# First token of each longer LSTM as seven block products instead of twelve plain ones, with VectorE's side work moved behind the first state

## The chip, the cores and the metric

One core of a Trainium2 chip runs the whole kernel. A core has five engines that each work through their own queue in order: TensorE (PE) multiplies 128x128 weight blocks with a stream of columns and writes to PSUM, VectorE (DVE) adds and multiplies elementwise, ScalarE (ACT) evaluates sigmoid, tanh and copies, GpSimd (POOL) does slower elementwise work, and SyncE (SP) issues DMAs. They wait for one another on semaphores. The metric is device time in microseconds (us); the kernel before takes 1878.06 us, the median of 3 runs (1877.81 to 1878.57).

## The reference, cut to what matters

Four residual layers work on x of shape (128 batches, 64 positions, 256 channels): a graph convolution with batch norms, then a graph convolution followed by windowed LSTMs, then two attention layers. The change concerns the LSTMs of the second layer alone:

```python
for p in range(1, MAX_SKIP + 1):                      # MAX_SKIP = 4
    nw = Tv // p
    wins = h[:, :nw * p, :].reshape(Bv * nw, p, Hd)
    last = _lstm_last(Wih[p-1], Whh[p-1], bih[p-1], bhh[p-1], wins)
    h = h.at[:, jnp.arange(nw) * p + (p - 1), :].set(last.reshape(Bv, nw, Hd))

def step(carry, x_t):                                 # in _lstm_last, from zero h and c
    h, c = carry
    g = x_t @ Wih.T + h @ Whh.T + bias
    i, f, gg, o = jnp.split(g, 4, axis=-1)
    c = sigmoid(f) * c + sigmoid(i) * tanh(gg)
    h = sigmoid(o) * tanh(c)
```

Positions are cut into windows of p tokens, an LSTM runs over each window, and its last state replaces the window's last position. The four LSTMs follow one another, since each reads what the one before wrote. At the first token h and c are zero, so only x_t @ Wih.T of the three gates i, g and o is needed.

## The kernel before

The 128 batches are worked on in eight pairs of chunks, "superchunks" sc = 0 to 7. Each holds 16 batches x 64 positions as a tile hT of 128 partitions x 2 channel blocks (k) x 1024 columns. For one superchunk the generator `lstms` runs p = 1 (`single`) and then `lstm` for p = 2, 3, 4. An LSTM with window p has n = 512, 336 or 256 columns for p = 2, 3, 4, and halves of m = n/2 = 256, 168 or 128 columns.

**Seven products.** A gate's 256x256 weight times its n columns is a 2x2 block product. The kernel already computes it for p = 1 and for all later tokens in Winograd's form of Strassen's method: seven products of 128x128 weights (or sums of weights) with m columns (or differences of columns) in place of eight, and some additions. The kinds are numbered 1 to 7. Kinds 1, 2 and 3 take columns as they are; 5, 6, 7 and 4 take the differences that `differences` makes (POOL for the x side in `operands_x`, VectorE for the h side, tile hd). The results are put together by copies (ScalarE, out of PSUM) and additions (VectorE, one operand out of PSUM). Weight sums are made once per (p, gate) in `weight_sums` (L744), kept in DRAM and loaded as tiles `wset` by `load_sets`; a set holds the x side, then the h side.

**The first token before** (L1106 to L1138) is the exception: for each of the gates 0, 2, 3 (i, g, o) and each output block c it sums two plain products (k = 0, 1) of n columns in its own PSUM bank: 12 products. All six with k = 0 come first, then a yield, then the six with k = 1. Six activations `first_acts` (L1113) read the banks, then come the cell c = 0 (L1119), its tanh (L1120), c = 1, and for each c the state h (`new_state`, L1093, tile hs). Between and behind the two states VectorE makes the h differences: dh[0] (L313) needs the state of c = 0 alone, dh[1] and dh[2] (L314 to L316) need both.

**The tokens after it** (class `Unit`, products at L1155, additions at L1164) start with the x parts of kinds 5, 3 and 2 for gates 0 and 2; after a yield come the h part of kind 5 (which reads dh[0]), copies, kind 1, and so on.

**Order of the work around it.** The order of instructions on each engine is written out by hand. PSUM has the tags x, y and z with two banks each for the LSTMs, and ps with two for everything else. `lstms` yields marks: a plain yield moves a counter n to the next whole number (a "tick"), a yield of "a" adds a half. In a superchunk p = 1 has ticks 0 to 3; p = 2 starts with 4 (in the middle of the first token's products) and 5 (after the x parts of the next token); p = 3 has 8 and 9 and p = 4 has 14 and 15 in these two places, and 21 is the end. At each tick the loop near the end of the LSTM part advances other generators by one step, as tuples of ticks say: CONV, BEGUN and FIRST (graph convolutions of coming chunks), RESIDUAL (adding the finished LSTM output, with a way through DRAM), AHEAD, LATE and FINAL (first norm of the attention layer), IDLE (idle transposes in the last superchunk, which has no convolutions).

The steps of a convolution that matter here, in order: scaled; transposes and DMA (L988, L247, L254, L995); add_squares (L284, VectorE, after that DMA); ln_stats (L159, L160); two applies (L196, ScalarE); aggregate "b" (L214, PE); two copies of its banks (L1005, VectorE); product_v (L915, PE, reads those copies); bounded (L921, VectorE); product_u (L929, PE, reads what bounded wrote); biased (L935, VectorE); aggregate "c" (L214, PE, reads what biased wrote); two steps of ScalarE (L940).

Before the change, for the chunk with an even number, both copies stand at tick 4 and product_v at tick 5; biased at tick 8 and aggregate "c" at tick 9. For the odd chunk bounded stands at tick 14 and product_u at tick 15. On VectorE, ticks 4, 8 and 14 lie ahead of everything of the first token but its products.

Of the kernel before, what the change touches and what calls it, by code (L numbers as in the profile page):

```python
# [13 lines left out]
P = 128  # L14
# [5 lines left out]
def kernel(  # L20
# [666 lines left out]
    with tc.manual_schedule(engines={mybir.EngineType.PE}):  # L687
# [56 lines left out]
        def weight_sums(p, q):  # L744
# [10 lines left out]
            far = dram.tile([P, 15, P], F32, tag=f"ws{p}{q}", name=f"wfar_{p}_{q}", bufs=1)  # L755
            nc.sync.dma_start(far[:, :9], w[:, :9])
            nc.sync.dma_start(far[:, 9:], w[:, 10:])
# [125 lines left out]
    def load_sets(n):  # L883
        for _ in range(min(n, len(coming))):
            p, q = coming.pop(0)
            wsets[p, q] = w1.tile([P, 15, P], F32, tag="wset", name=f"wset_{p}_{q}", bufs=6)
            nc.sync.dma_start(wsets[p, q], wfar[p, q])
# [136 lines left out]
    BLOCKS = {1: (0, 8), 2: (2, 9), 3: (7, 14), 4: (3, 10), 5: (4, 11), 6: (5, 12), 7: (6, 13)}  # L1024
# [14 lines left out]
    def operands_x(p, hv, name, s):  # L1039
# [3 lines left out]
        t = l1.tile([P, 7 * (T // 3) * NB], F32, tag="xd", name=f"xd_{name}_{s}", bufs=2)  # L1043
# [6 lines left out]
    def lstm(p, hv, name, follows, x1, ending):  # L1050
# [39 lines left out]
        def new_state(s, c, part, engine=nc.vector):  # L1090
# [6 lines left out]
            else:  # L1097
# [8 lines left out]
        ox = {1: x1}  # L1106

        banks = {(q, c): bank(f"g{q}_{name}_{c}", tag) for q, tag in ((0, "y"), (2, "z"), (3, "x"))
                 for c in range(KD)}
        def first_acts(*qs):  # L1110
            for q in qs:
                for c in range(KD):
                    nc.scalar.activation(  # L1113
                        columns_of(gate(q, c)),
                        natural(banks[q, c][:, :n].rearrange("p (w b) -> p w b", b=nb)),
                        AF.Tanh if q == 2 else AF.Sigmoid, bias=bs[:, q * KD + c : q * KD + c + 1])

        def first_cell(c):
            nc.vector.tensor_mul(cells[:, c, :n], gate(0, c), gate(2, c))  # L1119
            nc.scalar.activation(gate(2, c), cells[:, c, :n], AF.Tanh)  # L1120

        products = [(q, c, k) for k in range(KD) for q in GATES[:3] for c in range(KD)]
        for at, (q, c, k) in enumerate(products):
            if at == 6:
                yield
            nc.tensor.matmul(  # L1126
                banks[q, c][:, :n].rearrange("p (w b) -> p w b", b=nb), wsets[p, q][:, 2 * k + c, :],
                hv[:, k, : (nw - 1) * p + 1 : p, :], start=(k == 0), stop=(k == KD - 1))
# [961 lines left out]
```

## Time and profile before

| what | value |
|---|---|
| median of 3 runs | 1878.06 us |
| the profiled execution | 1879.19 us, its span 1877.4 us, granted TensorE clock 0.999 |
| PE busy | 1847.4 us, 98% of the span |
| DVE, ACT, POOL busy | 1245.6, 1014.0, 550.2 us |
| one middle superchunk (586 to 741 us) | 155.0 us, PE 153.58, DVE 103.33, ACT 86.63, POOL 36.19 us busy |
| first-token products (L1126), 576 records | 184.1 us busy, 474 ns mean |
| products of later tokens, x and y from differences of x (L1155) | 256.9 us and 77.5 us busy |

A product in fp32 stands in the trace as two records of matmul. The records overlap: a record's duration counts its way through the array, so the pace is read from the starts of neighbours. In the timeline, twelve records of 128x512 take 5.15 us to the start of the next group (429 ns each), and records of 128x256, 128x168 and 128x128 follow at 216, 142.5 and 111.7 ns. A group in the timeline shows its start, its length, engine, line, and in brackets the idle time before it with what ended it.

### The profile page before, as it was taken

To read this page: it belongs to the slowest core of one execution; us is meant where nothing else is said; L and a number is where in the kernel's file an instruction comes from. 1 tells how busy PE (TensorE), PEld (TensorE's weight loads), DVE (VectorE), ACT (ScalarE), POOL (GpSimd) and SP (SyncE) were. 2 spreads that over 40 slices of the span, in tenths; PEclk is the share of its full clock that TensorE was granted. 3 is DMA by queue.
4 is the path that set the end of the run, shared out by engine and by line. 5 is a ranking of instruction groups with operands and counts; after the bars stand their busy time and mean duration, and the time that the engine had idled before them with its cause. 6 is when DMAs were issued, how large, how long until landed. Compare 5 with 4: busy or idle time off the path is not lost.

```text
span 1877.4 us, 39077 instructions
## 1 busy us (share of the span) xinstructions
PE 1847.4 (98%) x15077; PEld 1476.8 (79%) x15077; DVE 1245.6 (66%) x3150; ACT 1014.0 (54%) x2284; POOL 550.2 (29%) x704
## 2 busy tenths in 40 slices
PE   8999989999999999999999999999999999999998
PEld 6877856895897798699589689778968967777776
DVE  6768855566577666667666766666565567776776
ACT  5766635556456456555655645655565544444453
POOL 5855722122222212212322312222132114332232
PEclk9999999999999999999999999999999999999999
DMA  3223652134334433332433443343144254444433
GB/s 115 71 70 141 238 200 92 66 129 152 107 130 147 145 141 127 113 136 95 150 119 132 165 137 130 130 132 125 60 142 140 70 157 136 145 149 139 144 113 114
DMA packets 111273, 241.45 MB, mean 129 GB/s; under 512 B 11504, under 2 KB 74864, under 8 KB 111088
## 3 DMA queue, kind: packets, MB, share of 16 engines
q1 hardware_dynamic: 110192, 237.09, 37.6%
q8 instruction: 119, 1.95, 0.4%
q0 software_dynamic: 320, 1.05, 0.2%
q10 hardware_dynamic: 576, 0.82, 0.1%
q14 instruction: 66, 0.54, 0.1%
HBM read 170.50 MB, written 68.42 MB: 127 GB/s over the span
## 4 chain that ended last, share of the span: by engine, by line
PE 86%; DVE 6%; DMA 2%; ACT 2%; issue 1%; POOL 1%; SPq 0%; DVEq 0%; ACTq 0%
PE x L1155 20%; PE z L1155 10%; PE g L1126 9%; PE v L1580 5%; PE y L1155 5%; PE x L1340 4%; PE y L1340 3%; PE v L915 3%; PE u L929 3%; PE p_q L1587 3%; PE X L1776 3%; PE X L423 2%; PE X L499 2%; PE Y L1776 1%; PE Y L423 1%
## 5 line engine op out<-in xcount | busy, mean ns | idle before, releaser
L1155 PE MATMUL x<-xd,wset 128*128 128x128 f32 (+2 forms) x1152 | 256.9, 305 | 8.6 <-DVE gates L1164 8.4
L1155 PE MATMUL x<-hd,wset 128*128 128x128 f32 (+2 forms) x1152 | 255.3, 303 | 0.0
L1221 POOL TENSOR_TENSOR gates<-gates 128x512 f32<-128x512 f32 (+2 forms) x48 | 75.2, 1566 | 534.4 <-ACT gates L1084 534.4
L1084 ACT ACTIVATE gates<-gates,bias 128x256 f32<-128x256 f32 (+4 forms) x384 | 172.4, 488 | 103.7 <-DVE gates L1164 103.7
L1164 DVE TENSOR_TENSOR gates<-gates,x 128x128 f32<-128x128 f32 (+2 forms) x384 | 120.7, 321 | 144.8 <-PE x L1155 141.6
L1164 DVE TENSOR_TENSOR gates<-gates,z 128x128 f32<-128x128 f32 (+2 forms) x384 | 102.6, 319 | 150.3 <-PE z L1155 150.1
L1155 PEld LDWEIGHTS x<-xd,wset 128*128 128x128 f32 x1152 | 188.2, 192 | 16.6 <-DVE gates L1164 11.6
L1155 PEld LDWEIGHTS x<-hd,wset 128*128 128x128 f32 x1152 | 188.5, 192 | 5.0
L1126 PE MATMUL g<-hT,wset 128*128 128x256 f32 (+2 forms) x576 | 184.1, 474 | 0.1
L1126 PEld LDWEIGHTS g<-hT,wset 128*128 128x128 f32 x576 | 108.6, 190 | 68.1 <-issue 37.8
L1161 ACT COPY gates<-y 128x128 f32<-128x128 f32 (+2 forms) x192 | 53.9, 293 | 197.4 <-PE y L1155 195.6
L1155 PE MATMUL z<-hT,wset 128*128 128x128 f32 (+2 forms) x768 | 146.7, 303 | 0.0
L1155 PE MATMUL z<-hs,wset 128*128 128x128 f32 (+2 forms) x768 | 146.5, 303 | 0.2 <-DVE hs L1093 0.2
L1155 PEld LDWEIGHTS z<-hT,wset 128*128 128x128 f32 x768 | 117.3, 191 | 3.7
L1155 PEld LDWEIGHTS z<-hs,wset 128*128 128x128 f32 x768 | 117.2, 191 | 3.6 <-DVE hs L1093 0.3
L1113 ACT ACTIVATE gates<-g,bias 128x512 f32<-128x512 f32 (+2 forms) x144 | 74.9, 560 | 38.1 <-PE g L1126 37.5
L1084 ACT ACTIVATE gates<-x,bias 128x128 f32<-128x128 f32 (+2 forms) x192 | 75.0, 390 | 30.1 <-PE x L1155 27.7
L1155 PE MATMUL x<-hT,wset 128*128 128x128 f32 (+2 forms) x384 | 86.0, 306 | 0.2 <-ACT gates L1084 0.2
L1155 PE MATMUL x<-hs,wset 128*128 128x128 f32 (+2 forms) x384 | 84.9, 303 | 0.0
L1236 ACT ACTIVATE gates<-cell 128x256 f32<-128x256 f32 (+2 forms) x144 | 55.2, 383 | 48.4 <-DVE cell L1235 48.4
L1155 PE MATMUL y<-hd,wset 128*128 128x128 f32 (+2 forms) x384 | 79.7, 310 | 0.0
L1155 PE MATMUL y<-xd,wset 128*128 128x128 f32 (+2 forms) x384 | 77.5, 304 | 1.8 <-ACT gates L1113 1.8
(326 smaller groups left out, 4120.9 us busy)
## 6 DMA issues: line engine op xcount, KB each, us to landing
wset<-wfar SPq DMA_DIRECT2D x96, 960.0 KB, 6.5
hT<-far_h SPq DMA_DIRECT2D x124, 128.0 KB, 3.1
far_h<-hm SPq DMA_DIRECT2D x16, 512.0 KB, 2.8
far_n<-xs SPq DMA_DIRECT2D x16, 512.0 KB, 3.5
xs<-far_n SPq DMA_DIRECT2D x64, 128.0 KB, 4.6
far_x<-xs SPq DMA_DIRECT2D x16, 512.0 KB, 3.0
x<-far_x SPq DMA_DIRECT2D x64, 128.0 KB, 3.2
xt<-in_x_dram SPq DMA_DIRECT2D x15, 512.0 KB, 4.0
```

The source lines that it names most:

```text
L423: nc.tensor.matmul(self.banks[tag][:, i * CH // 2 : (i + 1) * CH // 2], w, self.at[kind], start=first and not i, stop=True, skip_group_che ...
L915: nc.tensor.matmul(banks[m], wg0_sb[:, k, m * P : (m + 1) * P], agg[:, k, :], start=(k == 0), stop=(k == KD - 1))
L929: nc.tensor.matmul(banks[j // 2][:, j % 2, :], v[:, k, j * P : (j + 1) * P], wg1_sb[:, k, :], start=(k == 0), stop=(k == KD - 1))
L1084: nc.scalar.activation(gate(q, c, part), src, AF.Tanh if q == 2 else AF.Sigmoid, bias=bs[:, q * KD + c : q * KD + c + 1])
L1113: nc.scalar.activation(columns_of(gate(q, c)), natural(banks[q, c][:, :n].rearrange("p (w b) -> p w b", b=nb)), AF.Tanh if q == 2 else AF. ...
L1126: nc.tensor.matmul(banks[q, c][:, :n].rearrange("p (w b) -> p w b", b=nb), wsets[p, q][:, 2 * k + c, :], hv[:, k, : (nw - 1) * p + 1 : p, ...
L1155: nc.tensor.matmul(folded(self.psum(kind)), wsets[p, self.q][:, BLOCKS[kind][i], :], (ox[self.s] if part == "x" else oh)[kind], start=firs ...
L1164: nc.vector.tensor_add(gate(self.q, *dst), gate(self.q, *a), self.psum(kind))
L1221: nc.gpsimd.tensor_mul(gates[:, 0, :, :n], gates[:, 0, :, :n], gates[:, 2, :, :n])
L1340: nc.tensor.matmul(folded(ps(g, kind)), wih1[:, g, KINDS1[kind], :], right[kind], start=kind in (2, 5, 1), stop=True, skip_group_check=True)
L1580: nc.tensor.matmul(ps[:, i, :], hT[:, k, j, :], w[:, k, first : first + D], start=(k == 0), stop=(k == KD - 1))
L1776: nc.tensor.matmul(st[c, tag][:, i * CH // 2 : (i + 1) * CH // 2].rearrange("p (a n) -> p a n", n=P), w, st[c, "o7"][kind], start=first an ...
```

## The change

For p = 2, 3, 4 the first token is made of seven products as well. The class `First` holds one gate; `all_first` runs each step over the three gates. A gate has two banks: kinds 1 and 2 (and later 6, 7, 4 over kind 1's half) in one, 5 and 3 in the other, with the tags "yz", "yz", "xx". The x operands of token 0 are made by `operands_x` beside those of token 1 (four more POOL operations per LSTM), and the tile xd gets smaller and has three buffers in place of two. The second plain weight block is no longer needed, so a weight set shrinks from 15 to 14 blocks (three DMAs write it instead of two).

The yields of the first token are now: one after kinds 1 and 5, a half mark "a" behind the first state and dh[0], and the old one after the x parts of the next token, which now run in the order 3, 2, 5. The tuples of ticks change with it: what stood at ticks 4, 8 and 14 on VectorE now stands at 4.5, 8.5 and 14.5; add_squares of the odd convolution moves from 19 to 21; transposes of the second RESIDUAL from 2 to 1; several steps of AHEAD, FINAL and RESIDUAL move by one to four ticks.

```diff
-            far = dram.tile([P, 15, P], F32, tag=f"ws{p}{q}", name=f"wfar_{p}_{q}", bufs=1)
-            nc.sync.dma_start(far[:, :9], w[:, :9])
-            nc.sync.dma_start(far[:, 9:], w[:, 10:])
+            far = dram.tile([P, 14, P], F32, tag=f"ws{p}{q}", name=f"wfar_{p}_{q}", bufs=1)
+            for at, n, src in ((0, 1, 0), (1, 7, 2), (8, 6, 10)):
+                nc.sync.dma_start(far[:, at : at + n], w[:, src : src + n])
...
-        t = l1.tile([P, 7 * (T // 3) * NB], F32, tag="xd", name=f"xd_{name}_{s}", bufs=2)
+        t = l1.tile([P, 2 * CH], F32, tag="xd", name=f"xd_{name}_{s}", bufs=3)
...
-        products = [(q, c, k) for k in range(KD) for q in GATES[:3] for c in range(KD)]
-        for at, (q, c, k) in enumerate(products):
-            if at == 6:
-                yield
-            nc.tensor.matmul(
-                banks[q, c][:, :n].rearrange("p (w b) -> p w b", b=nb), wsets[p, q][:, 2 * k + c, :],
-                hv[:, k, : (nw - 1) * p + 1 : p, :], start=(k == 0), stop=(k == KD - 1))
-        first_acts(0, 2)
-        first_cell(0)
-        first_acts(3)
-        first_cell(1)
-        for c in range(KD):
-            new_state(0, c, every)
-            if not c:
-                dh[0]()
+        class First:
+            def __init__(self, q, tags):
+                self.q, self.ps = q, [bank(f"{t}{q}_{name}_{i}", t) for i, t in enumerate(tags)]
+            def psum(self, kind):
+                return self.ps[kind in (5, 3)][:, m:n] if kind in (2, 3) else self.ps[kind in (5, 3)][:, :m]
+            def product(self, kind):
+                nc.tensor.matmul(folded(self.psum(kind)), wsets[p, self.q][:, BLOCKS[kind][0], :], ox[0][kind],
+                                 start=kind in (1, 5), stop=True, skip_group_check=True)
+            def copy(self, c, j, kind):
+                nc.scalar.copy(gate(self.q, c, halves[j]), self.psum(kind))
+            def add(self, dst, a, kind):
+                nc.vector.tensor_add(gate(self.q, dst[0], halves[dst[1]]),
+                                     gate(self.q, a[0], halves[a[1]]), self.psum(kind))
+        firsts = [First(q, tags) for q, tags in ((0, "yz"), (2, "yz"), (3, "xx"))]
...
+        all_first(made(1), lambda u: u.copy(0, 0, 1), made(5), lambda u: u.copy(1, 1, 5))
+        yield
+        all_first(made(2), lambda u: u.add((0, 0), (0, 0), 2), made(3), made(6), lambda u: u.add((0, 1), (1, 1), 6),
+                  lambda u: u.add((0, 1), (0, 1), 3), made(7), lambda u: act(u.q, 0, every, gate(u.q, 0)),
+                  lambda u: u.add((1, 1), (1, 1), 7), made(4),
+                  lambda u: act(u.q, 1, halves[1], gate(u.q, 1, halves[1])))
+        nc.vector.tensor_mul(cells[:, 0, :n], gate(0, 0), gate(2, 0))
+        nc.scalar.activation(gate(2, 0), cells[:, 0, :n], AF.Tanh)
+        all_first(lambda u: act(u.q, 1, halves[0], u.psum(4)))
+        new_state(0, 0, every)
+        dh[0]()
+        yield "a"
+        nc.vector.tensor_mul(cells[:, 1, :n], gate(0, 1), gate(2, 1))
+        nc.scalar.activation(gate(2, 1), cells[:, 1, :n], AF.Tanh)
+        new_state(0, 1, every)
         dh[1]()
         dh[2]()
...
         A = [Unit(q, 1) for q in (0, 2)]
-        each(A, pe(5, "x"), pe(3, "x"), pe(2, "x"))
+        each(A, pe(3, "x"), pe(2, "x"), pe(5, "x"))
         yield
...
-                operands[p + 1] = operands_x(p + 1, hv, names[p + 1], 1)
+                operands[p + 1] = {s: operands_x(p + 1, hv, names[p + 1], s) for s in range(2)}
...
-    RESIDUAL = (0, 3, 4), (2, 5, 5.5)
-    CONV = (3, 4, 4, 5, 5.5, 7, 8, 9, 10, 10), (3, 4, 4, 11, 11.5, 13, 14, 15, 15.5, 17, 18, 20)
-    BEGUN = (11, 11, 13, 14, 16), (17, 17.5, 19)
...
-    AHEAD = (4, 5, 7, 12, 14, 15), (6, 7)
-    LATE = 5, 6, 8, 9
...
-    FINAL = (4, 5, 10, 12, 12, 14), (6, 7, 11, 14, 14, 16)
+    RESIDUAL = (0, 3, 5.5), (1, 5, 7)
+    CONV = (4, 4.5, 5, 5.5, 7, 8.5, 9, 10, 10), (3, 5, 5.5, 11, 11.5, 13, 14.5, 15, 15.5, 17, 18, 20)
+    BEGUN = (11, 11, 13, 15, 16, 17), (17, 17.5, 21)
...
+    AHEAD = (6, 7, 9, 12, 15, 19), (8, 9)
+    LATE = 5, 6, 9, 9.5
...
+    FINAL = (6, 7, 9.5, 10, 12, 13), (8, 9, 11.5, 12, 15, 15.5)
```

(FIRST, the tuple of the first superchunk, places the same steps at the same half ticks.)

## The prediction

> **What bounds the kernel now.** I read the page's busy times, then who waits for whom on PE, then the groups by form, then the timeline of one superchunk engine by engine.
>
> ```profile
> PE 1847.4 (98%) x15077; PEld 1476.8 (79%) x15077; DVE 1245.6 (66%) x3150; ACT 1014.0 (54%) x2284; POOL 550.2 (29%) x704
> ```
>
> ```profile
> PE x L1155 <- DVE gates L1164: 8.4, 13, 1.8
> ```
>
> ```profile
> L1126 PE MATMUL g<-hT,wset 128*128 128x512 f32 x192 | 85.6, 596 | 0.0
> ...
> L1126 PE MATMUL g<-hT,wset 128*128 128x336 f32 x192 | 55.7, 447 | 0.0
> ...
> L1126 PE MATMUL g<-hT,wset 128*128 128x256 f32 x192 | 42.8, 380 | 0.1
> ```
>
> PE is the bound: busy for 98% of the span; the second line, its largest group of waits, comes to 8.4 us in all. So a product saved is time saved, but every wait that the change puts in front of PE is lost in full. The last three rows are what is replaced: 192 records of each size in eight superchunks, 24 per LSTM.
>
> The timeline of superchunk 1 (start, length, group) shows how little air there is. PE first, then VectorE, for p = 2, 3 and 4:
>
> ```profile
> 450.12 5.31 PE L1126 MATMUL g<-hT,wset 128*128 128x512 f32 x12
> ...
> 464.30 3.60 PE L915 MATMUL v<-cv,wg_sb 128*128 128x512 f32 x8
> 467.73 1.03 PE L1155 MATMUL y<-hd,wset 128*128 128x256 f32 x4
> ...
> 492.77 6.94 PE L1126 MATMUL g<-hT,wset 128*128 128x336 f32 x24
> ...
> 501.35 1.16 PE L214 MATMUL agg_c<-adjt_bd,cv 64*64 64x64 f32 x64
> 502.44 0.84 PE L1155 MATMUL y<-hd,wset 128*128 128x168 f32 x4
> ...
> 537.48 5.34 PE L1126 MATMUL g<-hT,wset 128*128 128x256 f32 x24
> ...
> 544.00 3.62 PE L929 MATMUL u<-wg_sb,cv 128*128 128x256 f32 x16
> 547.46 0.61 PE L1155 MATMUL y<-hd,wset 128*128 128x128 f32 x4
> ```
>
> ```profile
> 456.64 1.29 DVE L1005 COPY cv<-agg_b 128x512 f32<-128x512 f32 x2 [0.32 <-PE agg_b L214]
> ...
> 464.56 0.43 DVE L313 TENSOR_TENSOR hd<-hs 128x256 f32<-128x256 f32 x1
> ...
> 496.10 1.25 DVE L935 TENSOR_TENSOR cv<-u,c 128x512 f32<-128x512 f32 x2
> ...
> 501.01 0.33 DVE L313 TENSOR_TENSOR hd<-hs 128x168 f32<-128x168 f32 x1
> ...
> 539.32 1.28 DVE L921 TENSOR_TENSOR cv<-v,nc 128x512 f32<-128x512 f32 x2
> ...
> 544.35 0.49 DVE L313 TENSOR_TENSOR hd<-hs 128x128 f32<-128x128 f32 x1
> ```
>
> The reader is to compare pairs. The copies, biased and bounded (L1005, L935, L921) are done 3.4 to 6.4 us before PE comes to the unit that reads them (product_v at 464.30, aggregate "c" at 501.35, product_u at 544.00). dh[0] (L313) ends at 464.99, 501.34 and 544.84: within 0.9 us of PE's reaching that unit, and the unit itself covers it.
>
> **What the Trainium skill says.** PSUM — Partial Sum Buffer, § PSUM bank collisions: accesses of two engines must be kept apart per bank, also for disjoint columns. So kind 7 has to wait for the addition that read kind 6, and kind 4 for the one that read kind 7. The trace agrees for the same pattern in later tokens (the stall of 1.18 us below), with 0.055 us from the addition's end to the next weight load and about 0.1 us more until PE is at its pace. Same page, § Engine vs sequencer instructions: VectorE's and ScalarE's queues are strict FIFO; the stall below shows it. VectorE: DVE Perf Modes, § The TRN2 errata: a fixed cost per instruction and (N+151)/0.96 ns for an fp32 addition, 291 ns at N = 128; this trace has 285, 327, 421 ns at 128, 168, 256. So halved additions are not half as dear.
>
> **Part 1: products.** Before, 24 records at 429, 282.5, 216 ns: 10.31, 6.78, 5.18 us. After, 21 products = 42 records at 216, 142.5, 111.7 ns: 9.06, 5.99, 4.69 us. Saved 1.25 + 0.79 + 0.49 = 2.53 us per superchunk, 20.2 us in all, if PE never waits.
>
> **Part 2: the new chain to the first state.** The product kinds run 1, 5, 2, 3, 6, 7, 4 over three gates. VectorE's order is add 2, add 6, add 3, add 7 (three each); ScalarE's is three activations of c = 0, three of half c = 1, tanh, three from PSUM of kind 4. Pace of neighbours: additions 0.20, 0.22, 0.33 us apart (p = 4, 3, 2), PSUM visible 0.19 us after a product's last slot, activations of n columns 0.40, 0.48, 0.61 apart, halves 0.29, 0.33, 0.42. I walk the queues from where PE starts the stage before.
>
> p = 4: PE starts at 537.48. Four kinds at 0.67 us: kind 6 begins at 540.16. Its third product + 0.19 + 0.28: add 6 ends at 541.30. Add 3 ends at 541.89, activations of c = 0 run from 541.54 to 542.78, the half ones free ScalarE at 543.61, tanh to 544.03, state (0.43) to 544.50, dh[0] to 544.84: the moment of before, though PE's own work ended 0.49 us earlier. Now bounded follows (tick 14.5), its halves ending at 545.43 and 546.03. product_u needs the second half for its second product: 546.09 + 0.1 + 14 records x 0.216 = 549.2, where before had 547.46: **1.74 us later**.
>
> p = 3: start 492.77, kind 6 at 496.19, add 6 to 497.57, activations 497.83 to 499.36, ScalarE free at 500.26, tanh 500.74, state 501.29, dh[0] 501.66; biased to 502.28 and 502.88. aggregate "c" starts at 502.34 in place of 501.35, its second half at 502.94; the h part of kind 5 follows at 503.6 in place of 502.44: **1.16 us later**.
>
> p = 2: start 450.12, kinds 1 and 5 (2.59), aggregate "b" (1.1), kinds 2 and 3 (2.59) and 0.2 us of waits for the copies, which ScalarE starts only after the last state of p = 1: kind 6 at 456.61. Add 6 to 458.51, activations 458.9 to 460.8, ScalarE free 461.99, tanh 462.62, state 463.35, dh[0] 463.81; copies to 465.02. product_v from 465.18 in place of 464.30, and kind 5 at 468.6 in place of 467.73: **0.87 us later**.
>
> Inside this lie waits at the banks (kind 4 waits for add 7, which stands behind three add 3): 0.75, 0.70, 0.79 us. They cost nothing extra, since PE then waits for VectorE's piece anyway; were the pieces elsewhere, these 2.24 us would remain of the 2.53 saved. I have 3.77 us per superchunk, within 0.3 us per LSTM either way, because the durations are measured but the paces mix forms. Seven superchunks: +26.4 us. In superchunk 0 the first token of p = 3 already waits 1.11 us (y from xd, for ACT L1113), which the new figure contains: -1.1.
>
> Superchunk 7 has no convolutions. With its idle transposes (4, 10, 8 records) p = 2, 3, 4 come out 0.87, 0.46, 0.84 us later (p = 2: kind 2 waits 1.2 us for the copies without aggregate "b" as cover). Against it, waits of 1.30, 0.74 and 0.74 us there end with moved steps. Together I take 0, bounds -1 and +2.
>
> **Part 3: add_squares from 19 to 21.**
>
> ```profile
> 731.70 1.29 DVE L284 TENSOR_TENSOR xs<-xs,cv 128x512 f32<-128x512 f32 x2 [1.40 <-DMA xs<-in_x_dram]
> 732.91 0.48 DVE L1164 TENSOR_TENSOR gates<-gates,x 128x128 f32<-128x128 f32 x2
> ```
>
> ```profile
> 733.24 0.49 PE L1155 MATMUL x<-xd,wset 128*128 128x128 f32 x2 [1.18 <-DVE gates L1164]
> ```
>
> VectorE waits for a DMA with PE's additions queued behind. At tick 21 the DMA has long landed, and 5.2 us of p = 1's products cover the 1.3 us. The stalls at this place are 0.69, 0.22, 1.18, 1.06 and 1.84 us: **-5.0 us**.
>
> **The rest at nothing.** Twelve more additions per LSTM (about 11 us per superchunk) fit VectorE's 51.7 us of idle time per 155; if not, the next step's additions are late. POOL's four extra differences end at about 540.2 for p = 4; kind 6 needs the third at 539.7 and starts at 540.16, so 0.45 us of air. ln_stats at ticks 9 and 15 (2.1 us) end before or within 0.2 us of the additions behind them, because PE is late itself. The transposes moved to tick 1 delay p = 1's additions by 0.8 us at most, under PE's products. SP: one more DMA per weight set in the first layer, moved puts and reorders each two ticks ahead of their reader; nothing waits for them unless a DMA takes over 8 us. Sets of 14 blocks load a little sooner.
>
> **Sum.** +26.4 - 1.1 - 5.0 + 0 = +20.3 us. Against the profiled execution, 1879.2 (span 1877.4), that is 1899.5; the median of runs is 1.1 us below it: **1898 us**.
>
> **Rivals.** (a) *Faster: VectorE's pieces are in time.* If activations and additions of different gates overlap more than my paces, the first delta is early and PE meets only the banks: -20.2 + 18 - 5 = -7, 1871; without the banks too, 1853. It decides from 0.85 us earlier in each of 24 stages. For it: VectorE idles before its additions in later tokens, and PE is 98% busy with the same product scheme there. Against: those have products of other gates between a kind and the next use of its bank; here there are none, and dh[0] lands no earlier than before in p = 3 and 4. 0.11. (b) *No change*: the chain is some 0.7 to 0.9 us shorter per stage and gain and waits cancel, 1878: 0.05. (c) *VectorE becomes late beyond the first token*: biased and bounded also push the second state back, ln_stats follows at once, and additions of the next step hold PE's banks by 0.5 us per LSTM more: +12, 1910. For it: three queues grow at one place. Against: PE reaches kind 3's h part at 550.5 in p = 4, the second state is there at 547.4. 0.10. That the order isn't what the change says can be left out: the built program has the seven kinds and the pieces where I put them.
>
> **Chances.** Forecast 0.74, its own range 1889 to 1906 (0.35 us per stage). For 8 in 10 I take 1880 to 1910, which leaves out (a) and the far end of (c). A change under 0.2% (3.8 us) can't be told from none. Slower 0.84, within 0.2% 0.05, faster 0.11.
>
> **What would show it.** Right: PE idle before L915, L214 (agg_c) and L929 at these places, released by VectorE's L1005, L935, L921, some 0.5 to 1.3 us each; PE idle before kind 4's products, released by the additions, 0.5 to 0.8 us; the stall at the end of p = 4 gone; PE's busy time down by up to 20 us in a longer span. Wrong: dh[0] ends over 0.8 us earlier than I have it, or PE shows no idle time ahead of those three units.

## The result, and the profile after

The kernel after takes 1921.62 us (median of 4 runs, 1920.72 to 1922.05) against 1877.93 for the kernel before on the same chip: a ratio of 1.0232, 95% interval 1.0214 to 1.025. The direction was as forecast, the size was not: +43.7 us in place of +20, beyond the end of the range.

The page of the kernel after, first part (busy time, share of the span, instructions):

```profile
span 1920.0 us, 40667 instructions
...
PE 1852.9 (97%) x15509; PEld 1515.9 (79%) x15509; DVE 1319.2 (69%) x3438; ACT 1052.4 (55%) x2500; POOL 607.1 (32%) x800
```

PE's busy time was to fall by up to 20 us. It rose by 5.5, although PE streams fewer columns. The profile gives a record more time than its place in the row: neighbours of 128x128 start 0.112 us apart, and one alone lasts 0.277 us. So up to 0.165 us of every delay of PE is booked as busy, and shorter delays show nowhere. There are many more of them: PE has 137 idle stretches above 0.05 us in place of 50. Idle time and busy time of PE both mislead here; the starts of the stages don't.

The waits of PE in the kernel after (engine, tile and line <- releaser: us in all, times, longest):

```profile
PE y L1116 <- DVE gates L1123: 10.8, 20, 0.7
PE x L1116 <- ACT gates L1358: 6.0, 8, 1.0
PE v L915 <- DVE cv L1005: 5.8, 7, 0.8
PE y L1169 <- ACT gates L1084: 4.8, 16, 0.4
PE agg_c L214 <- DVE cv L935: 4.2, 14, 0.3
PE x L1169 <- DVE gates L1178: 3.3, 8, 0.5
...
PE u L929 <- DVE cv L921: 2.5, 7, 0.4
```

L1116 is the product of the new first token, L1123 its addition, L1169 and L1178 those of later tokens. Rows 1, 3, 5 and 7 are the waits the prediction named. Row 6 (8.4 us before) no longer holds the stall at the end of p = 4, which is gone; it is a stop 12 us into that stage that was there before and grew from 0.24 to 0.46 us. Rows 2 and 4 it did not have: kind 1 of p = 2 waiting for the last activations of p = 1 (L1358), and the x part of kind 5 waiting for the bank that the first token's last activations (L1084) read.

Stage by stage, from the start of its first product to the start of the next stage's (a first token is counted up to the h part of kind 5, as in the prediction); us against the kernel before:

| stage | predicted | measured |
|---|---|---|
| p = 1, each of superchunks 1 to 6 | 0 | +0.37 |
| first token of p = 2, each | +0.87 | +1.97 |
| first token of p = 3, each | +1.16 | +1.69 |
| first token of p = 4, each | +1.74 | +1.82 |
| rest of p = 2 and of p = 3, each | 0 | 0.0 |
| rest of p = 4, superchunks 0 to 6 together | -5.0 | -6.0 |
| p = 1 and first tokens of superchunk 0 | +2.7 | +7.3 (p = 2 alone +5.2) |
| superchunk 7 | 0 | +4.5 |

The lines of measured values come to 41.0 us (5.85 x 6 + 7.3 + 4.5 - 6.0, and 0.1 in the rest of p = 3); the spans differ by 42.6, and 1.5 of it lies behind the last first token, where the code hardly changes (from there to the end: 409.9 us before, 411.4 after, 407.9 to 411.0 in the runs below).

The timeline of PE at the end of p = 4's first token, superchunk 1, kernel after:

```profile
551.74 0.71 PE L1116 MATMUL y<-xd,wset 128*128 128x128 f32 x4
552.29 0.39 PE L1116 MATMUL x<-xd,wset 128*128 128x128 f32 x2
553.07 0.68 PE L1116 MATMUL y<-xd,wset 128*128 128x128 f32 x4 [0.39 <-DVE gates L1123]
...
555.25 0.68 PE L1169 MATMUL y<-xd,wset 128*128 128x128 f32 x4 [0.38 <-ACT gates L1084]
556.30 1.95 PE L929 MATMUL u<-wg_sb,cv 128*128 128x256 f32 x7 [0.36 <-DVE cv L921]
```

Three stops within 3.3 us: kind 4 behind add 7 (kind 7 started at 551.74, its six records need 0.67, so the stop costs 0.66 and not the 0.39 shown), the x part of kind 5, product_u. The chain that PE waits for, on ScalarE and on VectorE:

```profile
552.37 2.18 ACT L1084 ACTIVATE gates<-gates,bias 128x256 f32<-128x256 f32 x6 [2.33 <-DVE gates L1123]
554.46 0.40 ACT L1143 ACTIVATE gates<-cell 128x256 f32<-128x256 f32 x1
554.76 0.60 ACT L1084 ACTIVATE gates<-y,bias 128x128 f32<-128x128 f32 x2
```

```profile
553.31 0.42 DVE L1142 TENSOR_TENSOR cell<-gates 128x256 f32<-128x256 f32 x1
554.89 0.43 DVE L1093 TENSOR_TENSOR hs<-gates 128x256 f32<-128x256 f32 x1 [1.16 <-ACT gates L1143]
555.35 0.29 DVE L313 TENSOR_TENSOR hd<-hs 128x128 f32<-128x128 f32 x1
555.56 1.28 DVE L921 TENSOR_TENSOR cv<-v,nc 128x512 f32<-128x512 f32 x2
```

The cell's product is done at 553.73; its tanh (L1143) starts at 554.46. In between ScalarE works off three activations of half c = 1, which nobody needs yet: they make up the second half of the group of six. Of VectorE's 1.16 us of idle time before the state, some 0.7 us is this, and the rest is tanh itself.

In p = 2 of superchunk 1 the trace of PE shows the stop that was not foreseen:

```profile
457.22 1.03 PE L1116 MATMUL y<-hT,wset 128*128 128x256 f32 x4
458.96 0.70 PE L1116 MATMUL x<-hT,wset 128*128 128x256 f32 x2 [0.72 <-ACT gates L1358]
```

### The profile page after: what moved, and what is told of

Its sections match the earlier page's. It is cut to its first block, busy times and chain, and to the rows that moved or that the text cites. A ratio compares the mean times of both kernels' runs of the same rounds, so it can differ in the third digit from the quotient of the medians.

```text
span 1920.0 us, 40667 instructions
## 1 busy us (share of the span) xinstructions
PE 1852.9 (97%) x15509; PEld 1515.9 (79%) x15509; DVE 1319.2 (69%) x3438; ACT 1052.4 (55%) x2500; POOL 607.1 (32%) x800
## 4 chain that ended last, share of the span: by engine, by line
PE 75%; DVE 10%; ACT 10%; issue 2%; POOL 2%; DMA 1%; SPq 0%; DVEq 0%; ACTq 0%; POOLq 0%
PE x L1169 22%; PE z L1169 9%; PE v L1593 5%; PE y L1169 5%; ACT gates L1084 3%; PE u L929 3%; PE v L915 3%; PE p_q L1600 3%; PE X L1789 3%; PE X L423 2%; PE X L499 2%; PE y L1116 2%; ACT gates L1358 2%; DVE gates L1123 1%; PE z L1116 1%
## 5 line engine op out<-in xcount | busy, mean ns | idle before, releaser
L1084 ACT ACTIVATE gates<-gates,bias 128x256 f32<-128x256 f32 (+4 forms) x528 | 235.0, 495 | 157.9 <-DVE gates L1178 88.3
L1169 PE MATMUL x<-xd,wset 128*128 128x128 f32 (+2 forms) x1152 | 256.6, 304 | 3.4 <-DVE gates L1178 3.3
L1169 PE MATMUL x<-hd,wset 128*128 128x128 f32 (+2 forms) x1152 | 254.7, 303 | 0.0
L1178 DVE TENSOR_TENSOR gates<-gates,x 128x128 f32<-128x128 f32 (+2 forms) x384 | 119.9, 320 | 122.2 <-PE x L1169 120.1
L1178 DVE TENSOR_TENSOR gates<-gates,z 128x128 f32<-128x128 f32 (+2 forms) x384 | 102.4, 318 | 137.4 <-PE z L1169 134.1
L1169 PEld LDWEIGHTS x<-xd,wset 128*128 128x128 f32 x1152 | 187.5, 191 | 10.4 <-DVE gates L1178 5.3
L1169 PEld LDWEIGHTS x<-hd,wset 128*128 128x128 f32 x1152 | 187.8, 191 | 4.9
L1169 PE MATMUL z<-hT,wset 128*128 128x128 f32 (+2 forms) x768 | 146.2, 303 | 0.0
L1169 PE MATMUL z<-hs,wset 128*128 128x128 f32 (+2 forms) x768 | 146.2, 303 | 0.0
L1175 ACT COPY gates<-y 128x128 f32<-128x128 f32 (+2 forms) x192 | 52.3, 289 | 143.3 <-PE y L1169 141.5
L1169 PEld LDWEIGHTS z<-hT,wset 128*128 128x128 f32 x768 | 117.2, 191 | 3.3
L1169 PEld LDWEIGHTS z<-hs,wset 128*128 128x128 f32 x768 | 117.1, 191 | 3.3
L1084 ACT ACTIVATE gates<-x,bias 128x128 f32<-128x128 f32 (+2 forms) x216 | 84.4, 391 | 29.4 <-PE x L1169 26.5
L1169 PE MATMUL x<-hT,wset 128*128 128x128 f32 (+2 forms) x384 | 85.9, 305 | 0.0
L1169 PE MATMUL x<-hs,wset 128*128 128x128 f32 (+2 forms) x384 | 84.9, 303 | 0.0
L1093 DVE TENSOR_TENSOR hs<-gates 128x256 f32<-128x256 f32 (+4 forms) x120 | 51.3, 427 | 46.6 <-ACT gates L1143 31.1
L1169 PE MATMUL y<-xd,wset 128*128 128x128 f32 (+2 forms) x384 | 78.5, 307 | 4.8 <-ACT gates L1084 4.8
L1608 POOL TENSOR_TENSOR s<-s,mx 128x256 f32<-128x256 f32 (+2 forms) x33 | 40.4, 1225 | 131.2 <-DVE mx L1607 123.5
L313 POOL TENSOR_TENSOR xd<-hT 128x128 f32<-128x128 f32 (+2 forms) x72 | 42.1, 585 | 124.5 <-DVE hT L1095 105.1
L1169 PE MATMUL y<-hd,wset 128*128 128x128 f32 (+2 forms) x384 | 79.2, 309 | 0.0
```

Source lines behind the costliest of these rows:

```text
L1084: nc.scalar.activation(gate(q, c, part), src, AF.Tanh if q == 2 else AF.Sigmoid, bias=bs[:, q * KD + c : q * KD + c + 1])
L1169: nc.tensor.matmul(folded(self.psum(kind)), wsets[p, self.q][:, BLOCKS[kind][i], :], (ox[self.s] if part == "x" else oh)[kind], start=firs ...
L1175: nc.scalar.copy(gate(self.q, kind // 5, halves[kind // 5]), self.psum(kind))
L1178: nc.vector.tensor_add(gate(self.q, *dst), gate(self.q, *a), self.psum(kind))
```

## The experiments

Ratios are against the kernel before, run on the same chip. The parts outside the eight superchunks differ by up to 3.5 us between runs, so small effects are read by stage, from the traces.

### Where the moved work went

One edit in each of two places, back to the ticks of before:

```diff
-    RESIDUAL = (0, 3, 5.5), (1, 5, 7)
+    RESIDUAL = (0, 3, 5.5), (2, 5, 7)
-    FIRST = ..., (1, 2, 4.5, 5, 6, 9, 11, ...)
+    FIRST = ..., (3, 3, 5.5, 7, 8, 8, 11, ...)
```

> The kernel after, with residual 1's transposes back at tick 2, and in superchunk 0 the second chunk's first six steps back at their old ticks (3, 3, 5.5, 7, 8, 8). Nothing else is changed. Theory M (moved work): the transposes at tick 1 push p = 1's additions and activations back, kind 1 of p = 2 then waits for the bank of p = 1's last activation. Then p = 1 loses its 0.37 us per superchunk, the first token of p = 2 goes from +1.97 to about +0.9 against the kernel before in superchunks 1 to 6, and in superchunk 0 from +5.2 to about +2: some -9.5 us, 1912. Theory C (the chain to the first state is longer than I walked it): p = 2 stays within 0.3 us of +1.97, and the total within 3 us of 1921.6.

1920.74 us, ratio 1.023 (1.0213 to 1.0247). p = 1 lost its 0.37 us as theory M has it, but the first token of p = 2 only 0.29, which by the numbers is theory C. The trace shows another reason than C's. The next three fences are from this run, p = 2 of superchunk 1: PE, ScalarE, VectorE.

```profile
464.53 1.13 PE L1116 MATMUL y<-hT,wset 128*128 128x256 f32 x4 [0.69 <-ACT gates L1120]
```

```profile
464.10 0.65 ACT L1120 COPY gates<-y 128x256 f32<-128x256 f32 x2 [1.39 <-DVE hT L1369]
```

```profile
459.37 2.11 DVE L1291 STREAM_TRANSPOSE hm<-hT 128x256 f32<-128x256 f32 x4
461.39 0.66 DVE L1363 TENSOR_TENSOR gates<-gates 128x512 f32<-128x512 f32 x1
461.96 0.69 DVE L1369 TENSOR_TENSOR hT<-hs,gates 128x512 f32<-128x512 f32 x1
462.82 1.20 DVE L1369 TENSOR_TENSOR hT<-cell,gates 128x512 f32<-128x512 f32 x1 [0.16 <-ACT gates L1366]
```

Kind 1's wait is gone, and kind 2 waits instead: for ScalarE's copy of kind 1, which writes the one buffer "gates" and so waits until VectorE's last state of p = 1 (ending 464.02) has read it. The transposes now stand ahead of that state. The old first token had no such link: it kept its sums in PSUM until its activations. In superchunk 0, with the restored ticks 7 and 8 (the second chunk's norm ahead of p = 3), the first token of p = 3 took 4.2 us more than in after; PE stood 3.62 us ahead of kind 6, for the additions (L1123). This second edit hides what the first one gained: the transposes at tick 2 alone save 0.67 us in each of superchunks 1 to 6, about 4 us.

So the transposes were taken out of p = 1 altogether, to tick 4.5, behind the first state of p = 2:

```diff
-    RESIDUAL = (0, 3, 5.5), (1, 5, 7)
+    RESIDUAL = (0, 3, 5.5), (4.5, 5, 7)
-    FIRST = ..., (1, 2, 4.5, 5, 6, 9, 11, ...)
+    FIRST = ..., (4.5, 4.5, 6, 7, 9, 9.5, 11, ...)
```

> The kernel after, with residual 1's transposes behind the first state of p = 2 (tick 4.5 in place of 1), and in superchunk 0 the second chunk's scaling and transposes at 4.5 and its next steps at 6, 7, 9, 9.5. At tick 2 (the run with the moves back) they held up p = 1's last state, behind which ScalarE's copies of kind 1 wait, and kind 2 then waited 0.69 us; at tick 1 they held up its last activations, and kind 1 waited 0.72 us. Theory M2 (both are the same 4 us of VectorE, and only a place outside p = 1 and ahead of no first token frees PE): p = 1 -0.37, p = 2 -1.0 to -1.3 us per superchunk against after, -8 to -10 us, 1912, and in superchunk 0 another -2 to -3. Rival N (they come back: 4 us of VectorE in s = 1 of p = 2 delay the additions of that step): the rest of p = 2 grows by 0.5 us or more, 1917 or above.

This kernel computes another residual for the second chunk of each superchunk: at tick 4.5 the transposes read hT after tick 3 has written the first chunk's residual into it. Instructions and shapes are the same. 1924.1 us, ratio 1.0246 (1.023 to 1.0261): p = 1 -0.37 and the first token of p = 2 -0.92 per superchunk, close to M2, but from superchunk 2 on the rest of p = 2 grew by 1.62, as rival N has it: PE waits there for ScalarE's copies (L1175; 6.9 us in all), which stand in ScalarE's queue behind a norm's activations (L196) that wait for VectorE. The tick-1 place was costing 1.3 us per superchunk. Tick 2 gives back half of it by stage (no run has that edit alone), tick 4.5 gives back all of it and loses more later. A place that is free in p = 1 and p = 2 both was not found.

### VectorE's pieces, and what stands ahead of the first tokens

```diff
-    CONV = (4, 4.5, 5, 5.5, 7, 8.5, 9, ...), (3, 5, 5.5, 11, 11.5, 13, 14.5, ...)
+    CONV = (4, 4, 5, 5.5, 7, 8, 9, ...), (3, 5, 5.5, 11, 11.5, 13, 14, ...)
```

(and the same in FIRST)

> The kernel after, with VectorE's copies, biased and bounded ahead of the first state as before (ticks 4, 8, 14 in place of 4.5, 8.5, 14.5), in superchunk 0 too. Theory P (the pieces behind the state are the price): PE's idle times before product_v, aggregate c and product_u (0.83, 0.60, 0.36 us) go, and with 3.5, 1.1 and 3.5 us of PE's work there the later state is partly covered: -0.8, -0.3, -0.4 us per superchunk, some -10 us, 1911. Theory Q (one queue: whatever stands ahead of add 6 on VectorE comes back as a longer wait at kind 4's bank): the three waits go, kind 4 and the h part of kind 5 wait by as much more, and the time stays within 4 us of 1921.6, or rises.

1915.4 us, ratio 1.0201 (1.0185 to 1.0216). Per superchunk the first tokens changed by -0.45 (p = 2), -0.04 and +0.07: the named waits went, and in p = 3 and p = 4 it all came back, as theory Q says, but at kind 6 and not at kind 4. In superchunk 1 PE stands 0.71 us (p = 3) and 0.62 us (p = 4) ahead of kind 6 until VectorE has made the first add 2, which now queues behind the piece (in p = 3 the trace names POOL's L313 there, which kind 6 doesn't read); kind 4 keeps its 0.49 and 0.39 us. Superchunk 0 gained about 1 us in p = 2 and in p = 3. The total lies between the two theories.

The other half, VectorE's unrelated work, moved away from the first tokens:

```diff
-    RESIDUAL = (0, 3, 5.5), (1, 5, 7)
-    CONV = (...), (3, 5, 5.5, ...)
-    BEGUN = (11, 11, 13, 15, 16, 17), ...
+    RESIDUAL = (0, 3, 5.5), (2, 5, 8.5)
+    CONV = (...), (4.5, 5, 5.5, ...)
+    BEGUN = (11, 11, 15, 15.5, 16, 17), ...
```

(AHEAD's and FINAL's second tuples follow one tick later, and FIRST's second has 4.5, 5, 7, 8.5, 9, 9 ahead of 11)

> The kernel after, with VectorE's unrelated work taken from directly ahead of the first tokens: ln_stats from tick 3 to 4.5, residual 1's transposes from 1 to 2 and its add_squares from 7 to 8.5, the add_squares of tick 13 to 15 with ln_stats at 15.5, and in superchunk 0 the second chunk's steps later (4.5, 5, 7, 8.5, 9, 9). The pieces stay behind the state. Theory M: what stands ahead of add 2 costs nothing, since VectorE idles 0.5 to 0.8 us before add 6 for PE; only the transposes count, as in the run before: -9.5 us, 1912, and p = 3 and p = 4 stay at +1.7 and +1.8. Theory D (VectorE starts the additions late in every first token): add 2 is done 1.0 to 1.5 us earlier, p = 3 and p = 4 drop to +1.0 or less, -20 us, about 1902.

1944.16 us, ratio 1.0352 (1.0337 to 1.0368), which neither theory had. By stage it is clear: the first tokens of p = 3 and p = 4 are the same to 0.01 us in the middle superchunks (one differs by 0.12), although an add_squares of 1.5 us no longer stands ahead of add 2. That decides for M and against D: VectorE was idle 0.5 to 0.8 us before add 6 in any case. The 22.5 us come from the new places: +1.77 in the rest of p = 2 (superchunks 2 to 6), +0.37 in that of p = 3 (6.0 in superchunk 0), +1.45 in that of p = 4.

Then the whole change without its products: the kernel before, its own 12 products, but after's ticks, a half tick behind dh[0], and c = 1's cell behind it.

```diff
         first_acts(0, 2)
         first_cell(0)
         first_acts(3)
+        new_state(0, 0, every)
+        dh[0]()
+        yield "a"
         first_cell(1)
-        for c in range(KD):
...
+        new_state(0, 1, every)
```

> The kernel before with its own first tokens (24 records per LSTM) but with all of after's ticks, and the half tick behind dh[0], so that the copies, biased and bounded stand behind the first state; sets of 15 blocks as before. It splits the change: pieces and ticks without the seven products. Theory P (the place of the pieces is the price): dh[0] ends as before, the pieces 1.2 us later, so product_v, aggregate c and product_u start some 2.0, 1.3 and 2.1 us later; less 8 us at the end of p = 4, that is +30 us against before, 1907; the seven products then cost another 14 us in place of saving 20. Rival K (the price is in the chain of the seven products): 1870 to 1882.

1886.72 us, ratio 1.0051 (1.0036 to 1.0066). That lies between the two theories, nearer to K. Per superchunk: p = 1 +0.37 (the transposes), first tokens +0.23, +0.95 and +1.09. Its waits of PE:

```profile
PE u L929 <- DVE cv L921: 4.6, 7, 0.7
PE agg_c L214 <- DVE cv L935: 4.0, 14, 0.3
```

There is no row for L915, and none at the banks of a first token. So the pieces and ticks cost 8.7 us, with gains of 7.4 us in the rest of p = 4 and 2.0 us in superchunk 7 in it, and putting the seven products in their place another 35 us, where by column count they save 20.

### ScalarE's order

```diff
                   lambda u: u.add((1, 1), (1, 1), 7), made(4),
-                  lambda u: act(u.q, 1, halves[1], gate(u.q, 1, halves[1])))
...
         nc.scalar.activation(gate(2, 0), cells[:, 0, :n], AF.Tanh)
-        all_first(lambda u: act(u.q, 1, halves[0], u.psum(4)))
+        all_first(lambda u: act(u.q, 1, halves[1], gate(u.q, 1, halves[1])),
+                  lambda u: act(u.q, 1, halves[0], u.psum(4)))
```

> The kernel after, with one order on ScalarE changed in the first token: tanh of the first cell ahead of the three activations of half c = 1, in place of behind them. Nothing moves on PE or VectorE. Theory S (ScalarE's three half activations, 0.9 to 1.3 us, stand between the cell's product and its tanh, and the first state is late by what they take): VectorE's wait before the first state (1.2 to 1.5 us) falls to 0.5, the pieces and the units that read them come 0.5 to 0.9 us earlier in p = 2 and 3, 0.3 to 0.4 in p = 4 (where the x part of kind 5 waits for ScalarE's last activations in either order): about -2.0 us per superchunk, -14 us, 1907. Rival T: the activations of kind 4 come later by the tanh (0.4 to 0.6 us), the bank of the next unit is free later, and the x part of kind 5 gives it back: within 4 us of 1921.6.

1907.69 us, ratio 1.0161 (1.0144 to 1.0178): the 14 us of theory S, with first tokens at -0.69, -0.77 and -0.59. In superchunk 7, which has no pieces to wait for, rival T holds: +0.9 us together. VectorE and ScalarE in p = 4 of this run (one line number less, L1141 is the cell and L1142 its tanh):

```profile
549.31 0.42 DVE L1141 TENSOR_TENSOR cell<-gates 128x256 f32<-128x256 f32 x1
550.22 0.43 DVE L1093 TENSOR_TENSOR hs<-gates 128x256 f32<-128x256 f32 x1 [0.48 <-ACT gates L1142]
```

```profile
549.77 0.42 ACT L1142 ACTIVATE gates<-cell 128x256 f32<-128x256 f32 x1
550.09 0.97 ACT L1084 ACTIVATE gates<-gates,bias 128x128 f32<-128x128 f32 x3
550.97 0.60 ACT L1084 ACTIVATE gates<-y,bias 128x128 f32<-128x128 f32 x2
```

From the cell's end to the state it is now 0.49 us in place of 1.16. The same edit together with the late transposes (and with their changed residual):

> The kernel after with both edits (the transposes at 4.5, tanh ahead of the half activations). If the two are separate, the sum of the two runs: -22 to -26 us, about 1897. If both free the same wait in p = 2, less by up to 0.8 us per superchunk: about 1903. Under T and N no better than 1915.

1908.49 us, ratio 1.0163 (1.0148 to 1.0178). The two add up in the first token of p = 2 (-1.61 = -0.69 - 0.92), so they are separate; but the late transposes give 1.5 us back in the rest of p = 2, and the total is no better than with tanh alone. My sum left that out.

Next, the activations out of PSUM ahead of the halves too, so that the bank is free sooner:

```diff
-        all_first(lambda u: act(u.q, 1, halves[1], gate(u.q, 1, halves[1])),
-                  lambda u: act(u.q, 1, halves[0], u.psum(4)))
+        all_first(lambda u: act(u.q, 1, halves[0], u.psum(4)),
+                  lambda u: act(u.q, 1, halves[1], gate(u.q, 1, halves[1])))
```

> The run with tanh first, and ScalarE's three activations of kind 4 (from PSUM) next, ahead of the three half activations. There PE waited three times per superchunk at the x part of kind 5 for the bank that these activations read (0.22, 0.44, 0.58 us, and up to 0.8 in superchunk 7). Theory V (behind this wait stands VectorE's piece anyway): the three waits go or shrink, and the waits for the copies, biased and bounded come back in their place; superchunks 0 to 6 gain 0 to 0.2 us in each first token, superchunk 7 (which has no pieces) 0.9 us: 1904 to 1907. Rival W (the bank is the bound): -0.5 us in each of 24 first tokens, -12, 1896.

1906.16 us, ratio 1.015 (1.0134 to 1.0165). Theory V: first tokens of the middle superchunks -0.09, +0.01 and -0.08, with L929 and L214 (agg_c) back in the list of waits. In superchunk 7 -0.44, -0.67, -0.86, twice what I expected.

### All three, and what remains

On top of that order, in p = 3 and p = 4 alone (FIRST's pieces likewise, AHEAD and FINAL following by a tick):

```diff
-    RESIDUAL = (0, 3, 5.5), (1, 5, 7)
-    CONV = (..., 7, 8.5, 9, ...), (..., 13, 14.5, 15, ...)
-    BEGUN = (11, 11, 13, 15, 16, 17), ...
+    RESIDUAL = (0, 3, 5.5), (1, 5, 8.5)
+    CONV = (..., 7, 8, 9, ...), (..., 13, 14, 15, ...)
+    BEGUN = (11, 11, 14.5, 15, 16, 17), ...
```

> The run before it, and in p = 3 and p = 4 of superchunks 0 to 6 also the pieces back ahead of the first token (ticks 8 and 14), with the add_squares that stood there moved behind it (7 to 8.5, 13 to 14.5), so that VectorE is free for the pieces while PE makes kinds 1 and 5. p = 2 as it is. If the three together (ScalarE's order, the pieces, VectorE's queue) are what eats the saving of the products, PE meets only the banks there: p = 3 and p = 4 each 0.6 to 0.8 us below the run with tanh first, about +0.2 to +0.5 us against the kernel before; -10 us, 1895. If the chain of the seven products itself (kind 6, its addition, add 3, three activations, product, tanh, state, difference) is longer than PE's work beside it, p = 3 and p = 4 stay within 0.2 us: 1904 to 1907. Moved add_squares may cost up to 0.4 us per superchunk in the rest of p = 3 or 4.

1895.19 us, ratio 1.0091 (1.0077 to 1.0105), as expected: against the run with tanh first, p = 3 -0.69 and p = 4 -0.82, and nothing lost in the rest of either. Edits that did nothing there alone (the pieces ahead, the queue cleared) pay together once ScalarE's order is out of the way; which of the two pays was not separated. PE in p = 4 of this run:

```profile
545.83 0.71 PE L1116 MATMUL y<-xd,wset 128*128 128x128 f32 x4
546.38 0.39 PE L1116 MATMUL x<-xd,wset 128*128 128x128 f32 x2
547.16 0.68 PE L1116 MATMUL y<-xd,wset 128*128 128x128 f32 x4 [0.40 <-DVE gates L1123]
...
548.79 0.61 PE L1169 MATMUL y<-xd,wset 128*128 128x128 f32 x4
549.24 2.97 PE L929 MATMUL u<-wg_sb,cv 128*128 128x256 f32 x13
```

In the first tokens of p = 3 and p = 4 one wait is left in superchunks 0 to 6, kind 4 behind add 7. Kind 7 follows kind 6 (544.99) by 0.84 us and kind 4 follows kind 7 by 1.33, where six records take 0.67: 0.83 us lost against 0.49 saved. That is +0.34 of the +0.41 us by which this stage is still longer than before (p = 3: +0.24, p = 2: +1.20 with kind 1's wait still in it). The prediction put this wait down to a rule of the Trainium skill's page "PSUM — Partial Sum Buffer", § PSUM bank collisions: two engines must be kept apart per bank, at disjoint columns too. The wait doesn't need that rule. In the code only kinds 1 and 5 start a sum; kinds 6, 7 and 4 are added onto kind 1 in the same columns, so each has to wait until VectorE has read the sum before it. Where the trace agrees with the page is the run with the pieces ahead: there kind 6 waits 0.62 us for add 2, which reads the other half of the bank. Between kind 7 and kind 4 of a gate stands only kind 7 of the other two gates. So in this order the products don't pay in the first token of p = 3 and p = 4 even with ScalarE's order, the pieces and the queue changed; another order of the additions (add 7 ahead of add 3, say) was not run.

### The ends, and the one part that pays

In superchunk 0, ln_stats of the first chunk one tick earlier and its two applies at 2 and 3; in superchunk 7, the ten idle transposes of p = 3 left out (they compute nothing).

```diff
-    FIRST = (1, 2, 3, 3, 4, 4.5, ...), ...
-    IDLE = {5: 4, 7: 18, 9: 10, 13: 14, 15: 8}
+    FIRST = (1, 1, 2, 3, 4, 4.5, ...), ...
+    IDLE = {5: 4, 7: 18, 13: 14, 15: 8}
```

> The kernel after with two edits in its end superchunks. In superchunk 0, ln_stats of the first chunk at tick 1 in place of 2 and its halves at 2 and 3 in place of both at 3: ScalarE applies them (2.1 us) ahead of the copies of kind 1, and they wait for VectorE and POOL. In superchunk 7, the ten idle transposes of p = 3 (1.1 us, ahead of the h part of kind 5, which dh[0] has freed by then) are left out; they compute nothing. Theory: the first token of p = 2 in superchunk 0 falls by 1.5 to 3 us, that of p = 3 in superchunk 7 by 0.9 to 1.1 us; about 1918.5. Rivals: superchunk 0 is POOL's differences alone (they wait for the last state in any case): under 0.5 us there; superchunk 7 waits for dh[0]: under 0.3 us there.

1920.94 us, ratio 1.0228 (1.0214 to 1.0242). Superchunk 7: p = 3 -1.09, so the filler had come to lie on the path. Superchunk 0: p = 2 -2.21, but p = 1 +2.23: PE now stands 2.35 us in p = 1 for its additions (L1377), ahead of which VectorE makes the norm's statistics, and kind 1 of p = 2 stands 2.58 us for p = 1's last activations (L1358), ahead of which ScalarE makes the two applies.

Part 3 alone, in the kernel before:

```diff
-    BEGUN = (11, 11, 13, 14, 16), (17, 17.5, 19)
+    BEGUN = (11, 11, 13, 14, 16), (17, 17.5, 21)
```

> The kernel before, with the add_squares of its tick 19 at tick 21; nothing else. It prices part 3 of the prediction alone. Theory: the five stalls of 0.2 to 1.8 us at the end of p = 4 go and nothing comes back: -5.0 us, 1873. Rival: the next p = 1 pays for it (its additions come later by up to 1.3 us, under PE's products or not): 0 to -2 us.

1870.56 us, ratio 0.9962 (0.9947 to 0.9977), and -8.3 us in the traces: -0.28 to -3.74 in each of superchunks 0 to 5, nothing anywhere else, so the rival falls. The medians of the runs differ by 6.4 us. The traces show more than theory's 5.0 for two reasons. The stalls shown as 0.69, 0.22, 1.18 and 1.06 us gave 0.96, 0.49, 1.45 and 1.34: each cost 0.27 us more than the idle time shown. And in superchunk 5 the kernel before lost another 1.6 us, because PE's granted clock was 0.50 for 3.4 us just after the 1.84 us stall (from 1197.9 us of the trace; records of 128x128 start 0.215 us apart there in place of 0.112). With after's ticks for the last superchunk as well:

```diff
-    FINAL = (4, 5, 10, 12, 12, 14), (6, 7, 11, 14, 14, 16)
+    FINAL = (6, 7, 9.5, 10, 12, 13), (8, 9, 11.5, 12, 15, 15.5)
```

> The kernel before with the add_squares at tick 21 (1870.6 us in its run, -8.3 us in the traces), and the last superchunk's steps (FINAL) at the ticks of after. In the run with old products and after's ticks, superchunk 7 was 0.6 us shorter in the rest of p = 3 and 1.4 us in the first token of p = 4. Theory: these 2.0 us come from FINAL alone: 1868.5. Rival: they come from the order of the first state: 1870.6, no change against that run.

1866.62 us (5 runs), ratio 0.9937 (0.9925 to 0.995): faster than both kernels. Superchunk 7 gains 1.61 in the rest of p = 3 and 1.45 in the first token of p = 4. The trace of this run, page and PE's waits:

```profile
PE 1843.2 (99%) x15077; PEld 1474.9 (79%) x15077; DVE 1254.3 (67%) x3150; ACT 1015.9 (54%) x2284; POOL 554.6 (30%) x704
```

```profile
PE x L1155 <- DVE gates L1164: 1.4, 6, 0.2
```

That row stood at 8.4, 13, 1.8 before.

## Why the prediction was off

**Right.** The bound and the mechanism: PE waits where pieces behind the first state are late, and kind 4 waits for add 7. p = 4 came out at +1.82 for 1.74. Part 3 came out at -6.0 for -5.0, but this is luck: the stalls were worth 8.3 us in the traces, 1.6 of it through the clock in superchunk 5, and the end of p = 4 keeps some 0.38 us more per superchunk in after (38.47 for 38.09), most of it in the stop of row 6. The bank waits were put at 0.75, 0.70 and 0.79 us and said to remain when the pieces are elsewhere: with all three edits 0.83 us remain in p = 4. POOL's extra differences held nothing up in p = 4. In p = 3 the trace names them as kind 4's releaser, but the first of add 7 ends at 507.77 us like POOL's last difference. The run with the pieces ahead settles it for add 7: POOL is done at 505.22 us there, the first of add 7 at 506.18, and kind 4 starts at 506.32 after the same 0.49 us. The difference named belongs to token 1, which kind 4 of the first token doesn't read.

**"The transposes moved to tick 1 delay p = 1's additions by 0.8 us at most, under PE's products."** This is the step that failed. They do delay the additions, and PE's products don't hide it: PE stops in p = 1 itself (0.14 us shown, for L1377), and p = 1 runs out of products. Behind the additions stand p = 1's last activations, which free the bank that kind 1 of p = 2 needs: 0.72 us shown, and with p = 1's own 0.37 about 1.3 us per superchunk (late transposes: -0.37 and -0.92), 7.7 us in six. Without the transposes there the first token of p = 2 is at +1.04 for the 0.87 of the forecast. The old first token hardly meets this wait: with these ticks and the old products p = 2 is at +0.23, while p = 1 has the same +0.37.

**p = 3, +1.16 for +1.69.** The chain to dh[0] was right to 0.15 us. Mis-sized was aggregate "c". I let half of it run between the two halves of biased; this is PE in the kernel after:

```profile
511.51 0.33 PE L214 MATMUL agg_c<-adjt_bd,cv 64*64 64x64 f32 x2 [0.33 <-DVE cv L935]
512.11 1.16 PE L214 MATMUL agg_c<-adjt_bd,cv 64*64 64x64 f32 x62 [0.27 <-DVE cv L935]
```

Two of 64 records can go ahead, 62 wait for the second half: about 0.4 us more than I took.

**Superchunk 0, +2.7 for +7.3.** I carried the middle superchunks' figure over. In after's trace p = 2's copies (301.51 us) follow a norm's applies on ScalarE (299.53 to 301.60), and POOL's first difference (297.33) follows that norm's two instructions (L99, L100); PE waits 2.24 us for the difference:

```profile
298.32 1.76 PE L1116 MATMUL z<-xd,wset 128*128 128x256 f32 x4 [2.24 <-POOL xd L313]
```

Neither was on the path to the first state before. Which of them costs what stays open, since moving the norm only moved the wait. Some 0.4 us is the clock: here too it was 0.50 for 3.4 us after the stop (the four records take 1.76 us for 1.03), and of the two runs with tanh and kind 4's activations first, which make p = 2 alike, the one without this (all three) is 0.43 us shorter in that stage.

**Superchunk 7, 0 for +4.5.** Its first tokens of p = 2, 3 and 4 wait for the copies with no convolution as cover (1.15, 0.67 and 0.49 us shown; I had it in p = 2 alone), kind 1 of p = 2 waits 0.96 us for p = 1's last activations wherever the transposes stand, and ten idle transposes that once filled a gap delay p = 3 by 1.09. Apart from the moved steps the first tokens came out 2.40, 1.99 and 2.18 us longer, for 0.87, 0.46 and 0.84; the moved steps gain 2.0 us (0.59 and 1.45, as in the run with the old products), for 2.8.

These terms make 7.7 + 3.2 (0.53 x 6) + 4.6 + 4.5 - 1.0 (the rest of p = 4) = 19.0 of the 20.7 us by which the stages differ from the forecast (41.0 less 20.3).

**What the forecast took as given.** I walked ScalarE's order as written, halves ahead of tanh, and got its length right; I did not ask whether the order was needed. It is worth 14 us, more than any wait on the list, and no view shows it as a wait of PE's: the trace names VectorE's L1005, L935 and L921 there.

## What to carry to other kernels

Before you count the columns that a product scheme saves, look at what stands between a product and the next one onto the same sum. Here it was 0.45 us of the other two gates in p = 4, and 0.49 us of saved columns became 0.83 us of waits. When results move from PSUM into a single SBUF buffer earlier than before, list who still reads that buffer: work that was hidden behind the stage before is now ahead of this one. And when a chain crosses two engines, check each queue for instructions that nobody awaits yet; a wait names only its last link, and edits that do nothing alone may pay once another link is shortened.

## What was not expected of the hardware

PE's busy time in a profile can rise while its work falls: it went from 1847.4 to 1852.9 us with 20 us fewer columns, because up to 0.165 us of each delay is booked as busy. A stop costs more than the idle time shown: kind 4's in p = 4 costs 0.66 us for 0.39 shown, and four stalls of the kernel before cost 0.27 us each beyond what was shown.

After a long stop the granted clock of TensorE can be at half for a while: 0.50 for 3.4 us after the 1.84 us stall of the kernel before, and after the 2.24 us stop in superchunk 0 of the kernel after. It is not certain: the run with tanh first has the same 2.24 us stop and no such stretch. What decides it no run here shows.

And additions with one operand out of PSUM come closer together than they last: three of 128x128 start 0.2 us apart in the kernel after (552.05 us, and 552.45 for the third), at 0.28 us each.
